# Third stage of a fused convolution block on one core: two tiling phases per chunk on TensorE, with six GELU buffers

## The chip, the cores and the metric

The kernel runs on one core of one Trainium2 chip. The metric is device time in microseconds. Before the change three runs took 3718.53, 3719.59 and 3721.88 us; the median is 3719.59 us. One further execution was recorded by the hardware profiler. All engines work in their own order of instructions: TensorE (PE, with its weight loads shown apart as PEld), VectorE (DVE), ScalarE (ACT), GpSimd (POOL) and SyncE (SP, which here only issues DMAs).

## The reference, cut to what matters

The input is 16 images of 192 channels and 64x64 pixels in float32. Layer 0 is a mixing block, layer 1 a convolution whose taps depend on the image:

```python
h = _ln2d(x, ln1_w, ln1_b)                      # layer norm over channels
projected, gate = split(conv1x1(h, in_proj_w))  # 192 -> 2 x 192
projected = dwconv3(projected, dw_k)
mixed = (directional_scan(projected) + dwconv3(projected, le_k)) * sigmoid(gate)
mixed = gelu(batch_norm(mixed))                 # statistics over all images
x = x + conv1x1(mixed, out_proj_w, out_proj_b)
h2 = _ln2d(x, ln2_w, ln2_b)
m = gelu(conv1x1(h2, fc1_w, fc1_b))             # 192 -> 768
x = x + conv1x1(m, fc2_w, fc2_b)                # 768 -> 192
# layer 1
pooled = x.mean(axis=(2, 3)); t = relu(norm(pooled @ w1.T)); wt = t @ w2.T + b2
out = depthwise_conv3(x, wt * MASK) + bias      # four taps are left by the mask
```

## The kernel before, in words

The kernel has three stages. The first projects x and writes the halves to DRAM, the second does the depthwise convolutions, the scans, the gate and the statistics of the batch norm. The third stage, which the change concerns, does the rest: the batch norm's GELU, the out projection with its residual, the second layer norm, the two products of the MLP, the pooling and layer 1.

The third stage works on pairs of images. Image 2p lies on partitions 0 to 63 and image 2p+1 on partitions 64 to 127; the 192 channels are three blocks t of 64. A chunk is 8 rows of 64 pixels, that is 512 pixels of each of the two images, so that a pair has 8 chunks (`NCH`) and all images together 64 (`n_ch`). Every engine's order is written out by hand (`tc.manual_schedule`); what stands in the loop is what each engine executes, in that order, and the framework only adds the semaphore waits that data and buffers require.

TensorE uses its array in two ways here. On quarters: weights of 64 rows and 64 columns, four products side by side, one for each combination of a 64-partition half of the input and a 64-partition half of the output. Over its full rows: weights of 128 rows and 64 columns, two products side by side. The products of one chunk n are these; a float32 matmul of the program is two MATMUL rows of the profile.

- `first` (line 980, quarters): fc1, 192 to 768 channels, six blocks m of 128 channels, 24 MATMUL rows each on 512 columns. A block goes to a PSUM tile of two banks with the tag `f1`, of which there are two; ScalarE applies the GELU to it (line 982) and writes a buffer `gl`, of which there are four.
- `second` (line 834, full rows): fc2, 768 to 192 channels, 36 pairs of MATMUL rows on 512 columns, accumulated over m into three PSUM banks with the tag `f2`.
- `out_quarters` (line 898, quarters) and `out_columns` (line 905, full rows): the out projection of channels 128 to 191 and 0 to 127 of chunk n+2, three blocks t of 8 MATMUL rows each on 256 columns. They go to half of an `f1` tile; `residual` (line 911, VectorE) adds x and the bias.
- `mean` (line 936, quarters): mean (`"sm"`) and mean square (`"sq"`) of chunk n+1 for the layer norm, 8 MATMUL rows each on 256 columns.

The loop runs over n. An iteration deals with chunk n in three rounds. Each round is `first(n, k)` on two blocks m, then `products(n, t)`, which takes one `f1` tile for one block t of the out projection of chunk n+2 and, for t 0 and 1, also for a mean of chunk n+1, and then one third of `second`. The third of `second` lags by one round, so that `second(n-1, 2)` stands in iteration n. Around these stand the other engines' steps: `center`, which subtracts the mean (VectorE, line 948); `squares`, one square on ScalarE (line 955) and five additions on VectorE (lines 956 and 928), into a buffer of its own; `normalize`, a square root on ScalarE with a table load before and after it (lines 964 and 966), a reciprocal (967) and a product (968) on VectorE; `final`, which adds fc2's result to the image (line 1000); `unmix`, three transposes on VectorE (line 239) of chunk n+3; `bn_gelu`, the batch norm's GELU on ScalarE (lines 861 and 862); `load` and `load_mixed`, DMAs that SP issues for chunks n+3 and n+4 (lines 204 and 227); and `piece`, called twice, which does one of the 12 output pieces of the pair that ended before (one activation on ScalarE, line 1039, three multiply-adds on VectorE, line 65, two DMAs on POOL, line 1043). After the last chunk of a pair, `pooled`, `squeeze` (line 1016) and `excite` (line 834, as `ps_k`) compute the taps of layer 1.

Of the kernel before, what the change touches and what calls it, by code (L numbers as in the profile page):

```python
# [21 lines left out]
F32 = mybir.dt.float32  # L22
# [33 lines left out]
def conv_block_kernel(ctx: ExitStack, tc: tile.TileContext, x, prm, w_in, w_out, w_fc1, b_fc1, w_fc2, w1, bn1, w2, out):  # L56
# [49 lines left out]
    pv = k2.tile([128, 2, NPRM], F32, tag="pv", name="pv")  # L106
# [58 lines left out]
    ones = ce.tile([128, 128], F32, tag="ones", name="ones")  # L165

# [697 lines left out]
    def products(n, t):  # L864


        if not -2 <= n < n_ch - 1:
            return
        ps = ps2.tile([128, 2, CH], F32, tag="f1", name="ps_o", bufs=2)
        pm, po = ps[:, :, HCH:CH], [ps[:, wh, 0:HCH] for wh in range(2)]  # L870
        if t < 2:
            at(mean, n + 1, pm, ("sm", "sq")[t])
        at(out_proj, n + 2, t, po)

        if t == 0:
            at(center, n + 1, pm)
        if t == 1 and 0 <= n + 1 < n_ch:
            st[n + 1]["pw"] = pm
        at(residual, n + 2, t, po)

# [12 lines left out]
    def out_quarters(n, t, ps, first_):  # L893
        s = st[n]

        for wh, qr in enumerate(HALF):
            for i, q in enumerate(HALF):
                nc.tensor.matmul(ps[wh][q], wo2[qr, 64 * t:64 * t + 64], s["mx"][qr, 2, 256 * i:256 * i + 256],  # L898
                                 start=first_, stop=not first_)

    def out_columns(n, t, ps, first_):
        s = st[n]
        for wh in range(2):
            for i, q in enumerate(HALF):
                nc.tensor.matmul(ps[wh][q].rearrange("p (r w) -> p r w", w=32), wo[:, 64 * t:64 * t + 64],  # L905
                                 cols(rows(s["mx"][:, i]))[:, :, wh], start=first_, stop=not first_)
# [23 lines left out]
    def mean(n, ps, what):  # L930


        s0, s1, sx = st[n][what]
        for k, kinds in enumerate(((s0, sx), (sx, s1))):
            for i, a in enumerate(kinds):
                nc.tensor.matmul(ps[HALF[i], k], mean64[HALF[k]], a[HALF[k]], start=True, stop=True)  # L936

    def mean_part(n, pm, t, k, src):

        for i, q in enumerate(HALF):  # L940
            nc.tensor.matmul(pm[q, k], mean64[q], src[q], start=(t == 0 and k == 0), stop=(t == 2 and k == 1))

    def center(n, pm):
        s, img = st[n], img_of(n)
        h = hp2.tile([128, 3, CH], F32, tag="h2", name="h2")
        hr = CR // 2
        for k in range(2):
            nc.vector.tensor_sub(h.rearrange("p t (h w) -> p t h w", w=HW)[:, :, k * hr:(k + 1) * hr], img[:, :, k * hr:(k + 1) * hr],  # L948
                                 rows(pm[:, k]).unsqueeze(1).broadcast_to([128, 3, hr, HW]))
        s.update(h=h)  # L950

    def squares(n):
        s = st[n]
        sq = wp.tile([128, 3, CH], F32, tag="sq2", name="sq2")
        nc.scalar.activation(sq, s["h"], AF.Square)
        nc.vector.tensor_add(sq[:, 0], sq[:, 0], sq[:, 1])
        v = sq.rearrange("p t (k n) -> p t k n", k=2)
        sums(v[:, 0, 0], v[:, 0, 1], v[:, 1, 0], v[:, 0, 0], v[:, 0, 1], v[:, 2, 0], v[:, 2, 1])
        s.update(sq=(v[:, 0, 0], v[:, 0, 1], v[:, 1, 0]))

    def normalize(n):
        s = st[n]
        rs = hp2.tile([128, CH], F32, tag="rs2", name="rs2", bufs=1)
        nc.scalar.activation(rs.rearrange("p (k n) -> p k n", k=2), s["pw"], AF.Sqrt, bias=eps6)  # L964

        nc.scalar.activation(warm, eps6, AF.Gelu)
        nc.vector.reciprocal(rs, rs)  # L967
        nc.vector.tensor_mul(s["h"], s["h"], rs.unsqueeze(1).broadcast_to([128, 3, CH]))  # L968

    def first(n, k):  # L970

        s = st[n]
        s["gl", k] = []
        for m in (2 * k, 2 * k + 1):
            pf = ps2.tile([128, 2, CH], F32, tag="f1", name="ps_f1", bufs=2)
            for t in range(3):
                for i, q in enumerate(HALF):
                    for j, o in enumerate(HALF):
                        m0 = 128 * m + 64 * j
                        nc.tensor.matmul(pf[o, i], wf1[q, t, m0:m0 + 64], s["h"][q, t], start=(t == 0), stop=(t == 2))  # L980
            gl = wp.tile([128, 2, CH], F32, tag="gl", name="gl", bufs=4)
            nc.scalar.activation(gl, pf, AF.Gelu, bias=bf1[:, m:m + 1])  # L982
            s["gl", k].append(gl)

    def second(n, k):
        s = st[n]
        if k == 0:
            s["po"] = [ps2.tile([128, CH], F32, tag="f2", name="ps_f2", bufs=3) for _ in range(3)]
        for j, gl in enumerate(s.pop(("gl", k))):
            m = 2 * k + j  # L990
            for t in range(3):
                both(s["po"][t], lambda i: wf2[:, m, 64 * t:64 * t + 64], lambda i: gl[:, i], m == 0, m == NFC - 1)
# [52 lines left out]
    def dynamic_last(p, g, t, dg, queues=(nc.gpsimd, nc.sync)):  # L1045
# [5 lines left out]
        else:  # L1051
            o = wp.tile([128, GR, HW], F32, tag="gl", name="ol", bufs=4)
# [36 lines left out]
    def out_alone(n, t, later=False):  # L1089

        if later:
            ps = [ps2.tile([128, CH], F32, tag="f2", name="ps_o2", bufs=3)[:, 0:HCH] for _ in range(2)]
# [8 lines left out]
    def one_bank():  # L1101
        return ps2.tile([128, 2, HCH], F32, tag="a", name="ps_m")
# [26 lines left out]
    load(2)  # L1129
    sq0 = wp.tile([128, 3, CH], F32, tag="sq2", name="sq2").rearrange("p t (k n) -> p k t n", k=2)  # L1130
# [8 lines left out]
    st[0]["pw"] = pw  # L1139
    normalize(0)  # L1140
# [4 lines left out]
    first(0, 0)  # L1145
    pm = ps2.tile([128, 2, CH], F32, tag="f1", name="ps_o", bufs=2)[:, :, 0:HCH]
    mean(1, pm, "sm")
    unmix(2)
    center(1, pm)
    bn_gelu(2)  # L1150
    squares(1)
    load(3)
    first(0, 1)
    unmix(3)
    out_alone(2, 0)
    second(0, 0)
    bn_gelu(3)
    products(0, 1)
    normalize(1)
    first(0, 2)  # L1160
    products(0, 2)
    second(0, 1)
    nc.vector.memset(pool2, 0.0)

    for n in range(1, n_ch + 1):
        ended = (n - 1) // NCH if n >= NCH and (n - 1) % NCH == NCH - 1 else None
        if n == 1:
            load_y(6, ys[3], (nc.gpsimd,))
        if n == NCH - 3:
            border(ximg[1])  # L1170
        at(load, n + 3)
        at(unmix, n + 3)
        at(load_mixed, n + 4)
        at(first, n, 0)
        at(bn_gelu, n + 3)
        products(n, 0)
        piece()
        at(squares, n + 1)
        at(second, n - 1, NPS - 1)
        at(final, n - 1)  # L1180
        if ended is not None:
            pooled(ended)
            if ended == n_pairs - 1:
                idle(2)
        at(first, n, 1)
        products(n, 1)
        if ended is not None:
            squeeze(ended)
        at(second, n, 0)
        piece()  # L1190
        at(normalize, n + 1)
        at(first, n, 2)
# [6 lines left out]
        products(n, 2)  # L1199
        at(second, n, 1)  # L1200

# [63 lines left out]
```

## Time and profile before

| | |
|---|---|
| runs | 3718.53, 3719.59, 3721.88 us (median 3719.59) |
| profiled execution, its own time | 3717.9 us |
| its span, first to last instruction | 3716.1 us |
| mean granted TensorE clock | 0.996 of full |
| busy: PE, DVE, ACT, POOL | 3693.1, 2700.6, 1784.8, 419.1 us |
| GELU on fc1's result (line 982) | 384 times, mean 1115 ns |
| first `first` of the third stage starts at | 1330.50 us |

How to read it: times are microseconds from the start of the span unless they are marked ns. A group of the page names line, engine, operation, the tile written, the tiles read, the shape and the count; then the busy time in total and the mean of one in ns, then the idle time of the engine just before these instructions and what ended most of it. "64\*64" in a MATMUL is the number of rows and columns of the array that it uses. A row of the timeline gives start, length, engine, line and operation of a run of equal instructions, and in brackets the idle time before it and what released it. Matmuls overlap: four quarter products that run side by side start some 7 ns apart, so starts, not lengths, tell what a group costs. What is true of a busy engine is not told by the share alone: a TensorE that is busy for 99% of the span can still lose time between two of its groups.

### The profile page before, as it was taken

How to read it: one execution, taken by the hardware profiler on the slowest of the kernel's cores; microseconds unless marked ns; L12 is line 12 of the kernel's file. 1: busy time of each engine (PE TensorE's matmuls, PEld its weight loads, DVE VectorE, ACT ScalarE, POOL GpSimd, SP SyncE). 2: the span in 40 equal slices, each digit the busy share in tenths (PEclk: the TensorE clock that was granted, in tenths of full speed). 3: DMA queues.
4: the chain of work that ended last, by engine and by line, in shares of the span. 5: the costliest groups of instructions: out<-in, count | busy, mean ns of one | idle time of the engine just before them, and what ended most of it. 6: DMA issues, size and time to landing. Idle time of an engine off the chain costs nothing.

```text
span 3716.1 us, 71125 instructions
## 1 busy us (share of the span) xinstructions
PE 3693.1 (99%) x30320; PEld 1649.0 (44%) x30320; DVE 2700.6 (73%) x4147; ACT 1784.8 (48%) x1940; POOL 419.1 (11%) x683
## 2 busy tenths in 40 slices
PE   9999999999999999999999999999999999999999
PEld 6666666555555533333333333333333333333333
DVE  7878776999999965557757756766675766675763
ACT  3334344888888843334434443434343443443433
POOL 3434342011011020000000000000000000000000
PEclk9999999999999999999999999999999999999999
DMA  7898997999999841112312222222222221221212
GB/s 170 253 253 247 262 282 259 284 297 283 283 281 271 225 101 39 40 44 69 84 48 68 72 62 67 63 65 64 72 57 62 77 68 46 78 74 43 69 38 74
DMA packets 289820, 491.80 MB, mean 132 GB/s; under 512 B 26456, under 2 KB 184144, under 8 KB 289504
## 3 DMA queue, kind: packets, MB, share of 16 engines
q1 hardware_dynamic: 232060, 296.09, 29.4%
q0 software_dynamic: 56512, 189.99, 18.5%
q8 instruction: 240, 3.93, 0.5%
q10 hardware_dynamic: 932, 1.16, 0.1%
q14 instruction: 76, 0.62, 0.1%
HBM read 284.95 MB, written 197.92 MB: 130 GB/s over the span
## 4 chain that ended last, share of the span: by engine, by line
PE 90%; DVE 1%; DMA 1%; ACT 0%; SPq 0%; issue 0%; POOL 0%; ACTq 0%; DVEq 0%
PE ps_f L980 27%; PE ps_f L834 27%; PE ps_l L668 11%; PE ps_pj L509 7%; PE ps_d L624 7%; PE ps_o L905 5%; PE ps_o L898 2%; PE ps_o L936 1%; PE ps_xt L480 1%; DMA xa<-in_x_dram 0%; PE ps_k L834 0%; PE ps_d L1067 0%; PE ps_i L1108 0%; DVE v L661 0%; PE pb_h L140 0%; DVE v L659 0%
## 5 line engine op out<-in xcount | busy, mean ns | idle before, releaser
L982 ACT ACTIVATE gl<-ps_f,bf 128x1024 f32<-128x1024 f32 x384 | 428.1, 1115 | 1318.1 <-PE ps_f L980 1318.1
L980 PE MATMUL ps_f<-h,wf 64*64 64x512 f32 x9216 | 1033.3, 593 | 3.0 <-DVE h L968 1.9
L834 PE MATMUL ps_f<-gl,place 128*64 128x512 f32 x4608 | 1022.2, 592 | 0.0
L980 PEld LDWEIGHTS ps_f<-h,wf 64*64 64x64 f32 x9216 | 333.6, 133 | 688.4 <-issue 633.7
L834 PEld LDWEIGHTS ps_f<-gl,place 128*64 128x64 f32 x4608 | 334.2, 137 | 574.5 <-issue 533.4
L509 PE MATMUL ps_pj<-wi,xa 64*128 64x384 f32 x3072 | 515.0, 487 | 1.1 <-DVE mid L514 0.9
L948 DVE TENSOR_TENSOR h<-ximg,ps_o 128x768 f32<-128x768 f32 x126 | 114.5, 950 | 420.7 <-PE ps_o L905 412.4
L509 PEld LDWEIGHTS ps_pj<-wi,xa 64*128 64x128 f32 x3072 | 292.1, 187 | 195.5 <-issue 10.6
L911 DVE SCALAR_TENSOR_TENSOR ximg<-ps_o,pt,low 128x256 f32<-128x256 f32 x384 | 167.8, 479 | 262.8 <-PE ps_o L905 259.1
L65 DVE SCALAR_TENSOR_TENSOR o<-ximg,taps,o 128x1024 f32<-128x1024 f32 x261 | 334.6, 1282 | 9.3 <-ACT o L1039 2.6
L1043 POOL DMA_DIRECT2D out_dram<-o x168 | 90.0, 541 | 2065.5 <-DVE o L65 2062.7
L967 DVE RECIPROCAL rs<-rs 128x512 f32<-128x512 f32 x64 | 214.3, 3349 | 28.6 <-ACT rs L964 28.6
L659 DVE TENSOR_TENSOR_SCAN v<-tab,q 128x1024 f32<-128x1024 f32 x96 | 218.3, 2274 | 7.8 <-DMA pg_d<-mid 7.8
L661 DVE TENSOR_TENSOR_SCAN v<-tab,q 128x1024 f32<-128x1024 f32 x96 | 217.5, 2265 | 0.0
L647 ACT ACTIVATE tab<-mask,dec_b 128x1024 f32<-128x1024 f32 x192 | 209.4, 1141 | 0.0
L905 PE MATMUL ps_o<-low,wo 128*64 128x256 f32 x1536 | 209.0, 393 | 0.0
L515 ACT ACTIVATE mid<-ps_pj,rsa 128x384 f32<-128x384 f32 x128 | 120.1, 939 | 185.0 <-PE ps_pj L509 176.6
L515 ACT ACTIVATE stg<-ps_pj,rsa 128x384 f32<-128x384 f32 x128 | 120.2, 941 | 179.0 <-PE ps_pj L509 172.5
L487 DVE BATCH_NORM_STATS2 st<-ps_xt 128x6 f32<-128x192 f32 x512 | 174.2, 340 | 11.8 <-PE ps_xt L480 10.9
L239 DVE STREAM_TRANSPOSE low<-low 128x512 f32<-128x512 f32 x174 | 167.8, 1016 | 2.1 <-issue 0.3
L1000 DVE SCALAR_TENSOR_TENSOR ximg<-ps_f,pt,ximg 128x512 f32<-128x512 f32 x192 | 134.4, 748 | 40.2 <-PE ps_f L834 37.8
L468 POOL DMA_DIRECT2D xa<-in_x_dram x192 | 119.8, 633 | 358.7 <-PE ps_pj L509 321.0
(210 smaller groups left out, 4050.4 us busy)
## 6 DMA issues: line engine op xcount, KB each, us to landing
low<-in_x_dram SPq DMA_DIRECT2D x128, 384.0 KB
out_dram<-o POOLq DMA_DIRECT2D x168, 256.0 KB, 3.7
mid<-pg_d SPq DMA_DIRECT2D x8, 4096.0 KB
low<-mixed_d SPq DMA_DIRECT2D x116, 256.0 KB
low<-pg_d SPq DMA_DIRECT2D x7, 4096.0 KB
pg_o<-pg_d SPq DMA_DIRECT2D x7, 4096.0 KB
xa<-in_x_dram POOLq DMA_DIRECT2D x192, 128.0 KB, 5.2
xa<-in_x_dram SPq DMA_DIRECT2D x192, 128.0 KB
```

Of the source, the lines that this page charges most:

```text
L65: nc.vector.scalar_tensor_tensor(o, in0, scalar, in1, ALU.mult, ALU.add, **kw)
L509: nc.tensor.matmul(ps[i], pixels(n, t, g)[q], wi[q, t].rearrange("p g k c -> p (g k c)"), start=(t == 0), stop=(t == 2))
L515: nc.scalar.activation(stag[blk][1][:, :, j], ps[1], AF.Copy, scale=rs[:, g, 1:2])
L624: nc.tensor.matmul(dst(ps[o, ih]), mats[g % 2]["dm"][q, di + 1, :, ch], src(s["pg"][q, :, 0, ch]), start=(di == 0), stop=stop)
L659: nc.vector.tensor_tensor_scan(vf, tab, q, 0.0, ALU.mult, ALU.add)
L661: nc.vector.tensor_tensor_scan(vf[:, ::-1], tab[:, ::-1], q[:, ::-1], 0.0, ALU.mult, ALU.add)
L668: nc.tensor.matmul(dst(bst[k]["ps"][o, i]), lm_of(g)[q, m, :, c], src(q, ih), start=start, stop=stop)
L834: nc.tensor.matmul(ps[q], w(i), rhs(i), start=start, stop=stop)
L905: nc.tensor.matmul(ps[wh][q].rearrange("p (r w) -> p r w", w=32), wo[:, 64 * t:64 * t + 64], cols(rows(s["mx"][:, i]))[:, :, wh], start=fi ...
L967: nc.vector.reciprocal(rs, rs)
L980: nc.tensor.matmul(pf[o, i], wf1[q, t, m0:m0 + 64], s["h"][q, t], start=(t == 0), stop=(t == 2))
L982: nc.scalar.activation(gl, pf, AF.Gelu, bias=bf1[:, m:m + 1])
```

## The change

An iteration of the loop becomes two phases. First all products on quarters: `first` for m 0 and 1, `mean` "sm" of chunk n+1, `first` for m 2 to 5, `mean` "sq", and `out_quarters` of chunk n+2 for all three t. Then all products over the full rows: `out_columns` for all three t, and the whole `second` of the same chunk n. `final(n-1)` stands at the head of the iteration, `normalize`, `residual` and `bn_gelu` stand between the phases, and `load`, `load_mixed` and `unmix` move behind the blocks of `first`.

Buffers go with it. `gl` has six buffers instead of four. The means no longer share an `f1` tile with the out projection; each takes two of the three `f2` banks (`two_banks`), and the square root is done in two halves. The out projection takes two `f1` tiles at once: t 0 and t 1 in the first halves of two tiles, t 2 in the second half of the first. The squares go to the x2 buffer of their chunk (`x2s[n % 2]`) instead of a buffer of their own, so that `load(n+3)` comes after the mean of the squares; `pv` moves to a pool that is closed before the third stage.

```diff
-    def products(n, t):
...
-        ps = ps2.tile([128, 2, CH], F32, tag="f1", name="ps_o", bufs=2)
-        pm, po = ps[:, :, HCH:CH], [ps[:, wh, 0:HCH] for wh in range(2)]
-        if t < 2:
-            at(mean, n + 1, pm, ("sm", "sq")[t])
-        at(out_proj, n + 2, t, po)
-
-        if t == 0:
-            at(center, n + 1, pm)
-        if t == 1 and 0 <= n + 1 < n_ch:
-            st[n + 1]["pw"] = pm
-        at(residual, n + 2, t, po)
...
     def squares(n):
         s = st[n]
-        sq = wp.tile([128, 3, CH], F32, tag="sq2", name="sq2")
+
+        sq = x2s[n % 2]
         nc.scalar.activation(sq, s["h"], AF.Square)
...
-        nc.scalar.activation(rs.rearrange("p (k n) -> p k n", k=2), s["pw"], AF.Sqrt, bias=eps6)
+        for k in range(2):
+            nc.scalar.activation(rs[:, k * HCH:(k + 1) * HCH], s["pw"][k], AF.Sqrt, bias=eps6)
...
-    def first(n, k):
+    def first(n, m):
...
+        pf = ps2.tile([128, 2, CH], F32, tag="f1", name="ps_f1", bufs=2)
+        for t in range(3):
+            for i, q in enumerate(HALF):
+                for j, o in enumerate(HALF):
+                    m0 = 128 * m + 64 * j
+                    nc.tensor.matmul(pf[o, i], wf1[q, t, m0:m0 + 64], s["h"][q, t], start=(t == 0), stop=(t == 2))
+        gl = wp.tile([128, 2, CH], F32, tag="gl", name="gl", bufs=6)
+        nc.scalar.activation(gl, pf, AF.Gelu, bias=bf1[:, m:m + 1])
+        s["gl", m] = gl
...
+    def two_banks(name):
+        return [ps2.tile([128, CH], F32, tag="f2", name=name, bufs=3)[:, 0:HCH] for _ in range(2)]
...
-    for n in range(1, n_ch + 1):
+    for n in range(n_ch + 1):
         ended = (n - 1) // NCH if n >= NCH and (n - 1) % NCH == NCH - 1 else None
-        at(load, n + 3)
-        at(unmix, n + 3)
-        at(load_mixed, n + 4)
-        at(first, n, 0)
-        at(bn_gelu, n + 3)
-        products(n, 0)
-        piece()
-        at(squares, n + 1)
-        at(second, n - 1, NPS - 1)
         at(final, n - 1)
...
+        at(first, n, 0)
         at(first, n, 1)
-        products(n, 1)
+        if n + 1 < n_ch:
+            pm = two_banks("ps_m")
+            mean(n + 1, pm, "sm")
+            center(n + 1, pm)
+        at(first, n, 2)
+        at(squares, n + 1)
+        for m in range(3, NFC):
+            at(first, n, m)
+        if n == 0:
+            unmix(2)
+            bn_gelu(2)
+        at(unmix, n + 3)
+        at(load_mixed, n + 4)
+        piece()
+        if n + 1 < n_ch:
+            st[n + 1]["pw"] = two_banks("ps_v")
+            mean(n + 1, st[n + 1]["pw"], "sq")
+        at(load, n + 3)
+        po = []
+        if n + 2 < n_ch:
+
+            pair = [ps2.tile([128, 2, CH], F32, tag="f1", name="ps_o", bufs=2) for _ in range(2)]
+            po = [[pair[j][:, wh, c0:c0 + HCH] for wh in range(2)] for j, c0 in ((0, 0), (1, 0), (0, HCH))]
+            for t in range(3):
+                out_quarters(n + 2, t, po[t], True, t < 2)
         if ended is not None:
             squeeze(ended)
+        for t in range(len(po)):
+            out_columns(n + 2, t, po[t], False, t > 0)
+        at(normalize, n + 1)
+        for t in range(len(po)):
+            residual(n + 2, t, po[t])
+        at(bn_gelu, n + 3)
         at(second, n, 0)
-        piece()
-        at(normalize, n + 1)
-        at(first, n, 2)
         if ended is not None:
             excite(ended)
...
-        products(n, 2)
         at(second, n, 1)
+        piece()
+        at(second, n, 2)
```

The lines ahead of the loop that did the first chunk apart are gone; the loop now begins at n = 0.

## The prediction

> **What bounds the kernel now.** I read the page first: shares, chain and groups.
>
> ```profile
> PE 3693.1 (99%) x30320; PEld 1649.0 (44%) x30320; DVE 2700.6 (73%) x4147; ACT 1784.8 (48%) x1940; POOL 419.1 (11%) x683
> ...
> PE 90%; DVE 1%; DMA 1%; ACT 0%; SPq 0%; issue 0%; POOL 0%; ACTq 0%; DVEq 0%
> ...
> L982 ACT ACTIVATE gl<-ps_f,bf 128x1024 f32<-128x1024 f32 x384 | 428.1, 1115 | 1318.1 <-PE ps_f L980 1318.1
> L980 PE MATMUL ps_f<-h,wf 64*64 64x512 f32 x9216 | 1033.3, 593 | 3.0 <-DVE h L968 1.9
> L834 PE MATMUL ps_f<-gl,place 128*64 128x512 f32 x4608 | 1022.2, 592 | 0.0
> ```
>
> TensorE is the chain, and in the third stage it waits for nobody: 3.0 us before all of `first`, nothing before `second`. So whatever an edit moves on VectorE, ScalarE or the queues counts only where it makes TensorE wait; and what can be saved must lie between TensorE's own groups. The timeline of TensorE in a chunk of the steady part shows what lies there.
>
> ```profile
> 2399.94 5.32 PE L834 MATMUL ps_f<-gl,place 128*64 128x512 f32 x24
> 2405.19 5.38 PE L980 MATMUL ps_f<-h,wf 64*64 64x512 f32 x48
> 2410.39 0.61 PE L936 MATMUL ps_o<-sq,mean 64*64 64x256 f32 x8
> 2410.82 0.61 PE L898 MATMUL ps_o<-low,wo 64*64 64x256 f32 x8
> 2411.36 1.08 PE L905 MATMUL ps_o<-low,wo 128*64 128x256 f32 x8
> 2412.28 5.32 PE L834 MATMUL ps_f<-gl,place 128*64 128x512 f32 x24
> ...
> 2436.52 4.03 PE L834 MATMUL ps_f<-gl,place 128*64 128x512 f32 x18
> ```
>
> Read start to start. A chunk takes 2436.52 - 2399.94 = 36.58 us. What do the groups cost without a change of tiling? The end of the stage, where two thirds of `second` follow each other, tells it:
>
> ```profile
> 3655.38 5.37 PE L834 MATMUL ps_f<-gl,place 128*64 128x512 f32 x24
> ...
> 3665.99 10.52 PE L834 MATMUL ps_f<-gl,place 128*64 128x512 f32 x48
> ```
>
> The second 24 rows add 5.15 us (0.429 a pair). In the steady part `second` takes 5.25 to the start of `first`: 0.10 more, at the change from full rows to quarters. `first`, whose 12 fours have the same pace, takes 5.20 to the mean that follows on quarters: 0.05 more, and the trace's starts put it between its first and second four (460 ns instead of 409). The mean takes 0.43, but `out_quarters`, equally large, 0.54: 0.11 at the change to full rows; `out_columns` then has 0.91 for four pairs of 0.215, another 0.05. A round trip between the two tilings therefore costs 0.10 + 0.05 + 0.11 + 0.05 = 0.31 us (0.312 with the trace's nanoseconds), three times a chunk. Check: 36.58 - 3 x 0.312 = 35.65, and 6 x 5.15 + 5 x 0.43 + 3 x 0.86 = 35.63.
>
> [...] after each change the first load starts together with its matmul and the next four is 0.05 late. The same would hold after any stop, and the one below shows it. [...] a block of `first` takes 2.57 us, its GELU 1.115. [...]
>
> **The change, part by part.** *Fewer changes of tiling.* In the order of TensorE's instructions I count the round trips in the third stage: 197 before (3 x 64, and 5 ahead of the loop), 76 after (64, the same 5, and 7 because `excite`, on quarters, now stands inside `second`). 121 x 0.312 = 37.8 us less. No matmul is added or left out.
>
> *A new wait in every chunk.* `f1` has two tiles. Blocks m 4 and m 5 of `first` fill the first and the second; then `out_quarters` wants the first for t 0 and the second for t 1. Between the last block and t 1 TensorE has only the mean (0.43) and t 0 (0.43). Call E the start of that mean. t 1 could start at E + 0.86, but the GELU of m 5 must have read the tile. The kernel before has this situation once, in its first chunk, where a block of `first` follows a single mean; the timeline of all engines there:
>
> ```profile
> 1335.70 0.61 PE L936 MATMUL ps_o<-sm,mean 64*64 64x256 f32 x8
> 1335.95 1.11 ACT L982 ACTIVATE gl<-ps_f,bf 128x1024 f32<-128x1024 f32 x1 [1.46 <-PE ps_f L980]
> ...
> 1337.11 5.38 PE L980 MATMUL ps_f<-h,wf 64*64 64x512 f32 x48 [0.80 <-ACT gl L982]
> ```
>
> TensorE resumes 1.41 us after the mean's start, 0.05 after the GELU's end. In the steady chunks the GELU starts a little later, since it waits for two semaphores:
>
> ```profile
> 2410.70 1.12 ACT L982 ACTIVATE gl<-ps_f,bf 128x1024 f32<-128x1024 f32 x1 [1.46 <-PE ps_f L980]
> ```
>
> That is E + 0.31 with E = 2410.39, so t 1 starts at E + 0.31 + 1.115 + 0.05 = E + 1.475. TensorE stands for 1.475 - 0.86 = 0.61 us, plus the 0.05 of a late second weight load: 0.66 a chunk. Nothing is done meanwhile: t 2, whose tile is free, and `out_columns` are queued behind t 1. Chunks 1 to 61 have it: 61 x 0.663 = 40.4 us. Bounds: with the faster start of the first chunk (0.25 instead of 0.31) and no late load it is 0.55, 33.6 us; with 0.1 us more it is 46.5. I take 40.4.
>
> *First chunk.* Its `bn_gelu(2)` stands behind the last GELU on ScalarE, and `out_quarters` needs it. In the trace the two activations end 1.83 us after the GELU before them, so the quarters start at E + 1.42 + 1.83 + 0.05 = E + 3.31 instead of E + 0.43: 2.9 us. The chunk before had stops of 1.03 (above) and 0.56 (TensorE resumes at 1356.82 instead of 1356.26, behind another GELU) which go. Net +1.3.
>
> *Chunk 62* has no out projection between the mean of the squares and `second`, and `second`'s second bank is the one that the square root reads. ScalarE has the GELU (to E + 1.42), the activation of the last piece (1.23, starting 0.1 early), the table load (1.28) and the root's first half: E + 4.33, of which I put 0.47 for half of a root that takes 0.69 whole. `second` wants the bank at E + 0.97: +3.4.
>
> *Where the same bank costs nothing:* in chunks 0 to 61 t 1 and t 2 of the quarters, 2.6 us of `out_columns` and the first pair of `second` lie between; the bank is wanted at E + 5.57 and the root's halves end at E + 4.3 and E + 4.8. With 1.2 us less of that cover each chunk would pay for what is missing.
>
> *VectorE*, chunk with pieces, from the chunk's start: the second piece of the chunk before ends 0.4 late, three `final` (0.83 each) end at 3, the mean asks for their banks at 5.25. `center` 6.1 to 7.9, square on ScalarE behind the third GELU to 11.1, five additions (0.69 + 1.77) to 13.6; the mean of the squares comes at E = 15.96: 2.3 spare. Transposes (2.9) to E + 0.6, piece (3.9) from E + 2.6 to E + 6.5, reciprocal 3.35 and product 1.76 to E + 11.7, residuals with their sums 5.3 to E + 17. The next chunk starts at E + 20.7, so that 3.7 are spare for its `f1` tiles and 9 for `h`; one more piece there would use up the 3.7. The square doesn't hold up the GELU of m 3, which can start only at 11.13.
>
> *Queues.* On SP `load(n+3)` goes behind `load_mixed`, eight DMAs whose issue takes 12.7 us, and behind the mean of the squares; it is used at E + 48. POOL's two DMAs a piece are the same. Splitting the root costs two fixed parts, 0.2 once ahead of the loop where nothing covers it (0 to 0.7). `pv` and the squares' buffer cost nothing: no instruction changes.
>
> Sum: -37.8 + 40.4 + 1.3 + 3.4 + 0.2 = +7.6 us. The profiled execution took 3717.9 us, 1.7 less than the median of the runs, so it is 3725.5 for that execution and 3719.6 + 7.6 = 3727.2 for the median.
>
> **The rivals.** *The wait is not there, or is hidden* (ends faster). If the GELU of m 5 were through by E + 0.86, only the other terms would count: 3719.6 - 37.8 + 4.9 = 3686.7. It decides in the time from the last block to t 1's tile: each 0.1 us less is 6.1 us, and below 0.42 of stop the kernel is faster by more than 0.2%. For it: the GELU's length and TensorE's resuming come from few places. Against: in 378 of the 384 cases ScalarE starts 0.72 after the block's last four starts, which is E + 0.31, and 0.61 of what follows would have to vanish. 8 in 100.
>
> *Another engine becomes late* (clearly slower). ScalarE or VectorE is behind in the chunks with pieces, 6 of 8, so that `second` waits for the root as well: past the 1.2 us of cover above, each 0.5 us more makes 46 x 0.5 = 23 us, 3750. For it: VectorE has 27 us of work in these chunks and a piece now stands ahead of the reciprocal. Against: the schedule above, where every meeting point has 1.2 us or more. 12 in 100.
>
> *The change doesn't do what it says*: the order of the changed program shows the two phases, so I give it nothing.
>
> **How the numbers follow.** The forecast has 80 in 100 and by itself lies between 3720 (the short wait, 0.55) and 3733 (the long one). 0.2% is 7.4 us, about what a measurement of this kernel can tell from no change, and the forecast's centre lies on it: of its 80, 38 fall within 0.2% and 42 slower. With the rivals: faster 8, within 38, slower 54. The range 3715 to 3741 holds the forecast's own and the beginning of the late-engine case.
>
> **What would show it.** Right: chunks of about 36.6 us as before; in each one 5 us long run of `out_columns` and `second` without a break; a new entry in the list of waits, TensorE at `ps_o` (`out_quarters`) for the GELU, 61 times some 0.6 us, 37 us in all; one wait of 3 us at chunk 0 and one at chunk 62 for the root. Wrong: no such entry and chunks of 35.96 us (first rival); TensorE waiting in `second` for the root, or for VectorE at a mean or `h`, in more than a chunk or two (second); or a round trip that costs something else where it is left, at `second` to `first` and at `out_quarters` to `out_columns`.

## The result, and the profile after

The changed kernel takes 3727.65 us (median of 13 runs, 3723.15 to 3731.02) where the kernel before takes 3718.56 us (median of 13, 3714.61 to 3721.88). The ratio of the times is 1.0023, with a 95% interval of 1.0016 to 1.0031: slower by a quarter of a per cent. The forecast was 3727.2, with 3715 to 3741 as its range. The medians differ by 9.1 us, where the prediction's sum gives 7.6; the interval, 5.9 to 11.5 us, holds both.

The page of the changed kernel, shares, chain and three of its groups (lines 963, 965 and 834 are `first`, its GELU and `second`):

```profile
PE 3666.2 (99%) x30320; PEld 1677.6 (45%) x30320; DVE 2703.6 (73%) x4147; ACT 1792.3 (48%) x2004; POOL 418.2 (11%) x683
...
PE 88%; ACT 2%; DVE 1%; issue 1%; DMA 0%; SPq 0%; ACTq 0%; POOL 0%; DVEq 0%
...
L965 ACT ACTIVATE gl<-ps_f,bf 128x1024 f32<-128x1024 f32 x384 | 427.4, 1113 | 1340.6 <-PE ps_f L963 1334.6
L963 PE MATMUL ps_f<-h,wf 64*64 64x512 f32 x9216 | 1014.9, 590 | 2.0 <-DVE h L953 2.0
L834 PE MATMUL ps_f<-gl,place 128*64 128x512 f32 x4608 | 1001.9, 592 | 2.8 <-ACT rs L949 2.8
```

TensorE's busy time fell by 26.9 us, from 3693.1 to 3666.2, and yet the execution is longer. ScalarE, at 0% of the chain before, now holds 2% of it. `second`, which waited for nobody, has one wait of 2.8 us. Which instruction waits for ScalarE the rest of the time is told by the list of TensorE's waits (tile, line, releaser: total us, times, longest):

```profile
PE ps_o L881 <- ACT gl L965: 26.3, 61, 0.4
...
PE ps_f L834 <- ACT rs L949: 2.8, 1, 2.8
PE ps_o L881 <- ACT low L862: 2.6, 1, 2.6
```

The out projection on quarters (line 881) waits for the GELU in 61 chunks; that is the entry that the prediction named, with its count. The other two are chunk 62 and chunk 0. The list has 0.4 us a time where the stop is 0.6, because it measures from the end of the matmul before, and that end is modelled some 0.2 us late. The starts tell it. TensorE's timeline in the chunk that corresponds to the one shown of before:

```profile
2400.11 5.38 PE L963 MATMUL ps_f<-h,wf 64*64 64x512 f32 x48
2405.31 0.61 PE L919 MATMUL ps_m<-sm,mean 64*64 64x256 f32 x8
2405.74 10.48 PE L963 MATMUL ps_f<-h,wf 64*64 64x512 f32 x96
2416.04 0.61 PE L919 MATMUL ps_v<-low,mean 64*64 64x256 f32 x8
2416.47 0.61 PE L881 MATMUL ps_o<-low,wo 64*64 64x256 f32 x8
2417.52 1.09 PE L881 MATMUL ps_o<-low,wo 64*64 64x256 f32 x16 [0.43 <-ACT gl L965]
2418.54 2.81 PE L888 MATMUL ps_o<-low,wo 128*64 128x256 f32 x24
2421.18 15.62 PE L834 MATMUL ps_f<-gl,place 128*64 128x512 f32 x72
2436.73 3.66 PE L963 MATMUL ps_f<-h,wf 64*64 64x512 f32 x32
```

A chunk takes 2436.73 - 2400.11 = 36.62 us; before it took 36.58. There is one change to full rows (2418.54) and one back (2436.73) where there were three of each. Between t 0 of the quarters (2416.47) and t 1 (2417.52) lie 1.05 us for work of 0.43, so TensorE stands for 0.62. ScalarE in the same place:

```profile
2416.35 1.11 ACT L965 ACTIVATE gl<-ps_f,bf 128x1024 f32<-128x1024 f32 x1 [1.46 <-PE ps_f L963]
2417.36 1.23 ACT L1022 ACTIVATE o<-ximg,pt,taps 128x1024 f32<-128x1024 f32 x1
...
2419.91 0.84 ACT L949 ACTIVATE rs<-ps_v,eps 128x256 f32<-128x256 f32 x2
```

The GELU of m 5 starts 0.31 us after the mean, ends at 2417.46, and t 1 starts 0.06 later. So in 61 chunks two round trips between the tilings were exchanged for one stop of nearly the same price: 36.583 - 2 x 0.312 + 0.663 = 36.622, which is what the chunk takes in the trace's nanoseconds.

Two executions are best compared from the first `first` of the third stage on, since what lies ahead of it ended between 1328.7 and 1336.2 us in the executions of this study, while its work differs by the split root alone. From there to the end the kernel before takes 2385.6 us and the changed one 2392.7: 7.1 more. By the prediction it is 7.4, its 7.6 less the 0.2 of the split root, which lies ahead of the loop.

### The profile page after: what moved, and what is told of

It reads as the page before. It is cut to its first block, busy times and chain, and to the rows that moved or that the text cites. A ratio compares the mean times of both kernels' runs of the same rounds, so it can differ in the third digit from the quotient of the medians.

```text
span 3721.4 us, 71304 instructions
## 1 busy us (share of the span) xinstructions
PE 3666.2 (99%) x30320; PEld 1677.6 (45%) x30320; DVE 2703.6 (73%) x4147; ACT 1792.3 (48%) x2004; POOL 418.2 (11%) x683
## 4 chain that ended last, share of the span: by engine, by line
PE 88%; ACT 2%; DVE 1%; issue 1%; DMA 0%; SPq 0%; ACTq 0%; POOL 0%; DVEq 0%
PE ps_f L963 27%; PE ps_f L834 27%; PE ps_l L668 11%; PE ps_pj L509 7%; PE ps_d L624 7%; PE ps_o L888 5%; PE ps_o L881 2%; ACT gl L965 2%; PE ps_xt L480 1%; PE ps_m L919 1%; PE ps_k L834 0%; PE ps_d L1050 0%; DMA out_dram<-ol 0%; PE ps_i L1095 0%; DVE v L661 0%
## 5 line engine op out<-in xcount | busy, mean ns | idle before, releaser
L963 PE MATMUL ps_f<-h,wf 64*64 64x512 f32 x9216 | 1014.9, 590 | 2.0 <-DVE h L953 2.0
L834 PE MATMUL ps_f<-gl,place 128*64 128x512 f32 x4608 | 1001.9, 592 | 2.8 <-ACT rs L949 2.8
L963 PEld LDWEIGHTS ps_f<-h,wf 64*64 64x64 f32 x9216 | 346.3, 133 | 627.9 <-issue 566.0
L931 DVE TENSOR_TENSOR h<-ximg,ps_m 128x768 f32<-128x768 f32 x128 | 116.4, 951 | 278.5 <-PE ps_m L919 277.3
L940 DVE TENSOR_TENSOR low<-low 128x512 f32<-128x512 f32 x63 | 43.6, 692 | 212.0 <-ACT low L939 212.0
L888 PE MATMUL ps_o<-low,wo 128*64 128x256 f32 x1536 | 181.6, 384 | 0.0
```

The lines of the kernel that those rows point to most:

```text
L834: nc.tensor.matmul(ps[q], w(i), rhs(i), start=start, stop=stop)
```

## The experiments

All kernels of this section are the changed kernel with the edit shown (of "no wait" and "all waits" a part, with the rest in words), and compute the whole reference. "Chunk" is the time from one `first` of m 0 to the next in the middle of the stage; "stage" is from the first `first` to the end of the profiled execution, of which there is one for each kernel. "E" is, as in the prediction, the start of the mean of the squares. The intervals are against runs of the kernel before on the same chip.

| kernel | us, median (lowest to highest, runs) | against before, 95% | chunk | stage |
|---|---|---|---|---|
| before | 3718.56 (3714.61 to 3721.88, 13) | | 36.583 | 2385.6 |
| changed | 3727.65 (3723.15 to 3731.02, 13) | 1.0023 (1.0016 to 1.0031) | 36.622 | 2392.7 |
| t 1 last | 3703.68 (3700.76 to 3709.73, 4) | 0.9962 (0.9947 to 0.9977) | 36.190 | 2368.3 |
| t 1 first | 3727.82 (3723.92 to 3731.61, 10) | 1.0025 (1.0015 to 1.0034) | 36.62 | 2392.8 |
| mean last | 3754.71 (3751.59 to 3756.89, 4) | 1.0096 (1.0079 to 1.0112) | 37.053 | 2421.2 |
| no wait | 3684.62 (3681.43 to 3685.01, 4) | 0.9907 (0.9892 to 0.9922) | 35.960 | 2351.9 |
| three trips | 3727.76 (3723.13 to 3731.73, 12) | 1.0023 (1.0015 to 1.0032) | 36.583 | 2392.4 |
| batch norm ahead | 3742.13 (3738.65 to 3743.83, 4) | 1.0062 (1.0047 to 1.0077) | 36.90 or 36.62 | 2407.0 |
| chunk 0 alone | 3725.76 (one run) | | 36.62 | 2390.9 |
| all waits | 3677.43 (3671.34 to 3681.70, 4) | 0.9888 (0.9873 to 0.9902) | 35.960 | 2345.1 |

The theory: TensorE takes its matmuls in the order written, and one stop before t 1 gives back what fewer changes of tiling save. The first question is whether the stop sets the time, which a stop of another length answers, and whether a round trip costs 0.31 us, which a kernel with a different number of trips answers. The rival: something else in the two phases (the order of VectorE, a late buffer) keeps the chunk at 36.6 us, and the wait is only where TensorE is seen to idle; then the time moves on to the next wait when this one is shortened.

### t 1 last

```diff
-            for t in range(3):
+            for t in (0, 2, 1):
                 out_quarters(n + 2, t, po[t], True, t < 2)
```

t 2 uses the second half of t 0's tile, so it can go ahead of t 1 and covers 0.43 us of the GELU.

> The order of the out projection's quarters is t 0, t 2, t 1 instead of t 0, t 1, t 2. Theory (a fixed wait for the GELU of block m 5): t 1 is reached 0.43 us later, at E + 1.29 instead of E + 0.86, and still released at E + 1.475, so the stop shrinks from 0.61 to 0.18 us a chunk: 61 x 0.43 = 26 us less than the changed kernel's 3727.7, that is 3701, ratio to the kernel before 0.9955. Rival (the tilings' round trips never cost what the trace suggests and the wait only takes place of another loss): no change beyond noise, 3727.

The chunk takes 36.190 us, 0.432 less. The list of waits has no entry for line 881 and the GELU any more; the timeline of TensorE shows what is left of the stop:

```profile
2405.97 0.61 PE L919 MATMUL ps_v<-low,mean 64*64 64x256 f32 x8
2406.40 1.71 PE L881 MATMUL ps_o<-low,wo 64*64 64x256 f32 x24
2408.03 2.81 PE L888 MATMUL ps_o<-low,wo 128*64 128x256 f32 x24
```

The 24 rows take 1.63 us to the next group, where three times 0.43 and the 0.11 of the change to full rows are 1.40. A stop of 0.18 and 0.05 of a late weight load are still in it, too short for the list because of the modelled ends. One line's order is worth 61 x 0.432 = 26.4 us, of which 1.7 were lost again at chunk 62 in the profiled execution (last section; 24.4 in the stage); the kernel is now faster than before. The rival falls for this step: nothing else caught the time.

### t 1 first

```diff
-            for t in range(3):
+            for t in (1, 0, 2):
                 out_quarters(n + 2, t, po[t], True, t < 2)
```

> The order of the quarters is t 1, t 0, t 2. Theory: t 1 is reached at E + 0.43 and released at E + 1.475, a stop of 1.04 us a chunk, 61 x 0.43 = 26 us more than the changed kernel: 3754, ratio to before 1.0095. Rival: 3727.

This expectation was missed, and the trace says why: the edit did nothing. TensorE's timeline:

```profile
2424.17 0.61 PE L881 MATMUL ps_o<-low,wo 64*64 64x256 f32 x8
2425.22 1.09 PE L881 MATMUL ps_o<-low,wo 64*64 64x256 f32 x16 [0.43 <-ACT gl L965]
```

There are eight rows without a wait, then the same wait, and 16 rows. So the tile that is written first had the buffer that came free first, that of m 4, whatever its name is. This fits a pool that gives out a buffer when a tile is first used and not when it is asked for; the profile shows no addresses, so it is read from the waits. The two tiles were renamed, not exchanged. What it gives is a repeat of the changed kernel, 1.0025. To lengthen the stop, something else had to be taken from its cover.

### Mean last

```diff
             st[n + 1]["pw"] = two_banks("ps_v")
-            mean(n + 1, st[n + 1]["pw"], "sq")
-        at(load, n + 3)
...
             for t in range(3):
                 out_quarters(n + 2, t, po[t], True, t < 2)
+        if n + 1 < n_ch:
+            mean(n + 1, st[n + 1]["pw"], "sq")
+        at(load, n + 3)
```

The mean of the squares, 0.43 us, stands behind the quarters, so that only t 0 lies between m 5 and t 1.

> In the run with t 1 first the tile of block m 5 was still the one used second, since a buffer is given out at its first use; so that run was the changed kernel under other names. Here the mean of the squares, 0.43 us, moves behind the quarters of the out projection, and the second tile is reached 0.43 us earlier. Theory: the stop grows from 0.61 to 1.04 us a chunk, 61 x 0.43 = 26 us more than the changed kernel: 3754, chunks of 37.05 us, ratio to before 1.0095. The rival, that the position in the queue doesn't matter: 3727.

The list of waits and the timeline of TensorE:

```profile
PE ps_o L881 <- ACT gl L965: 52.6, 61, 0.9
```

```profile
2432.12 0.61 PE L881 MATMUL ps_o<-low,wo 64*64 64x256 f32 x8
2433.59 1.09 PE L881 MATMUL ps_o<-low,wo 64*64 64x256 f32 x16 [0.86 <-ACT gl L965]
```

Between the first two starts lie 1.47 us, again 0.43 of work, so the stop is 1.04. The chunk takes 37.053 us, 0.431 more than in the changed kernel. Together with "t 1 last" and the changed kernel this is a dose: stops of 0.18, 0.61 and 1.04 us give chunks of 36.190, 36.622 and 37.053.

### No wait

```diff
-            pair = [ps2.tile([128, 2, CH], F32, tag="f1", name="ps_o", bufs=2) for _ in range(2)]
-            po = [[pair[j][:, wh, c0:c0 + HCH] for wh in range(2)] for j, c0 in ((0, 0), (1, 0), (0, HCH))]
-            for t in range(3):
+            pair = ps2.tile([128, 2, CH], F32, tag="f1", name="ps_o", bufs=2)
+            po = [[pair[:, wh, c0:c0 + HCH] for wh in range(2)] for c0 in (0, HCH)]
+            po.insert(1, two_banks("ps_o1"))
+            for t in (1, 0, 2):
                 out_quarters(n + 2, t, po[t], True, t < 2)
```

t 1 goes to two `f2` banks instead of m 5's tile, t 0 and t 2 to m 4's tile. For this the mean of the squares takes one `f2` bank and one bank that was idle; and since `second` needs the `f2` banks soon, `out_columns` and `residual` begin with t 1, and the first `piece` goes behind that residual. No matmul, activation or transfer is added.

> t 1 of the out projection goes to two f2 banks instead of the second f1 tile, comes first, and its residual is done first; the mean of the squares takes one f2 bank and the bank with the tag a. Theory: no wait for the GELU in any chunk, chunks of 35.96 us, 61 x 0.663 = 40.4 us less than the changed kernel: 3687, ratio to before 0.9915. The first bank of the second product is now the root's; it is wanted at E + 4.47 and free at E + 4.38, so at most a few tenths of a us in the 42 chunks with a piece may come back. Rival (the saved round trips were worth less than 0.312 us each): the kernel lands at the time before, 3719.

```profile
2400.83 1.48 PE L881 MATMUL ps_o<-low,wo 64*64 64x256 f32 x24
2402.23 2.81 PE L888 MATMUL ps_o<-low,wo 128*64 128x256 f32 x24
2404.87 15.62 PE L834 MATMUL ps_f<-gl,place 128*64 128x512 f32 x72
```

The timeline has the 24 rows at 1.40 us, nothing between them, and `second` follows at once; the list of waits has no entry for the GELU. The chunk takes 35.960 us, 0.662 less than in the changed kernel: 0.61 of stop and 0.05 of late weight load, the two parts that the prediction gave it. 61 x 0.662 is 40.4, and the wait for the root at chunk 62 became 0.9 shorter as well; the stage is 40.8 us shorter, and the medians differ by 43.0, which is the same within the intervals. The saving of the two round trips is there in full when the stop is gone, 1.0% in all.

### Three trips

```diff
             for t in range(3):
                 out_quarters(n + 2, t, po[t], True, t < 2)
+                out_columns(n + 2, t, po[t], False, t > 0)
         if ended is not None:
             squeeze(ended)
-        for t in range(len(po)):
-            out_columns(n + 2, t, po[t], False, t > 0)
```

Each t goes through both of its tilings before the next, so that the chunk has three round trips again. t 1 is then wanted 1.56 us after t 0's first row, which hides the GELU. Quarters and columns of a t follow each other as in the kernel before; all else is as in the changed kernel.

> The changed kernel with out_columns of each t right behind its out_quarters: three round trips a chunk again instead of one, and t 1 is reached only after the first out_columns, at E + 1.9, after its tile is free. Theory: + 2 x 0.312 us for the trips, - 0.663 us for the wait, so -0.04 us x 61 = 2 us less than the changed kernel: 3725, ratio to before 1.0017. If the trips cost nothing: 3687. If the wait were not what the GELU makes it: 3766.

```profile
2418.25 0.61 PE L881 MATMUL ps_o<-low,wo 64*64 64x256 f32 x8
2418.79 1.08 PE L888 MATMUL ps_o<-low,wo 128*64 128x256 f32 x8
2419.81 0.66 PE L881 MATMUL ps_o<-low,wo 64*64 64x256 f32 x8
```

The changes cost what they did in the kernel before: 0.54 for the eight quarter rows with the change to full rows, 1.02 for four pairs with the way back. The chunk takes 36.583 us, 0.623 more than without a wait and with one trip. Both of these kernels wait for nobody in a steady chunk, and two trips are the difference: 0.312 each. So the price of a trip, read from the gaps of the kernel before, holds here too.

The two prices now stand measured apart. Two trips cost 0.623 us, the stop 0.662. The change gains the first and pays the second.

### Batch norm ahead of the root

```diff
+        at(bn_gelu, n + 3)
         at(normalize, n + 1)
         for t in range(len(po)):
             residual(n + 2, t, po[t])
-        at(bn_gelu, n + 3)
```

This tests the second rival of the prediction, a late root. The cover is the time between the end of the root's first half and the moment at which `second` wants that bank. The two activations of `bn_gelu` here stand ahead of the root and take from it. The expectation already counts with a cover of 6.0 - 4.33 = 1.67 us instead of the prediction's 1.2, for a reason told below.

> The changed kernel with the batch norm's GELU of chunk n+3 (1.93 us on ScalarE) ahead of the square root instead of behind it. Theory, from the changed kernel's own trace: the root's first half ends at E + 4.33 with a piece ahead of it; now at E + 6.26, and the second product wants the bank at E + 6.0, so it stops for 0.26 us and 0.05 of wake-up and 0.05 of a late load in the 41 chunks with a piece there, none in the others: 15 us more than the changed kernel, 3742, ratio to before 1.0065. Rival (ScalarE already is at the edge, so that all 1.93 us come through in these chunks): 3807. Rival (ScalarE has ample room): 3727.

ScalarE's timeline, and TensorE's in the same chunk:

```profile
1686.88 1.23 ACT L861 ACTIVATE low<-low,bn_bi,bn_sc 128x1024 f32<-128x1024 f32 x1
...
1688.83 1.28 ACT L949 ACT_TABLE_LOAD   x1
1690.12 0.84 ACT L949 ACTIVATE rs<-ps_v,eps 128x256 f32<-128x256 f32 x2
```

```profile
1689.57 15.90 PE L834 MATMUL ps_f<-gl,place 128*64 128x512 f32 x72
```

`second` takes 15.90 us instead of 15.62: a stop of 0.23 and 0.05 of a late load are inside it. The first half of the root ends at E + 6.18 instead of E + 4.34, 1.84 later, and TensorE goes on at E + 6.23 where the changed kernel wants the bank at E + 6.00. So the cover in the changed kernel is 6.00 - 4.34 = 1.66 us, and it doesn't wait there. The expected 0.36 was too large by 0.08, because it moved the root by 1.93. The chunks with both a piece and a batch norm ahead of the root take 36.90 us, the others 36.62, since without the piece's 1.23 us there is room. There are 40 of them, not the 41 expected: chunk 61 has a piece, but no batch norm. Of the 14.3 us by which the stage is longer, 40 x 0.28 = 11.2 are this; 1.7 lie in chunk 62 and 1.3 at the end, both from TensorE's clock (last section).

### Chunk 0 alone

```diff
             mean(n + 1, pm, "sm")
+            if n == 0:
+                unmix(2)
             center(n + 1, pm)
...
             at(first, n, m)
-        if n == 0:
-            unmix(2)
-            bn_gelu(2)
+            if n == 0 and m == 3:
+                bn_gelu(2)
```

In the changed kernel chunk 0 cost more than the prediction gave it. This edit lets chunk 2's transposes and batch-norm GELU run earlier, so that chunk 0 has no stop for them and its products are the same.

> The changed kernel with the batch norm's GELU of chunk 2 between the blocks of first of chunk 0, nothing else. Chunk 0 of the changed kernel takes 40.33 us: 2.8 of stop and some 1.4 more, in which the products after the stop run at half their pace. Theory (a stop of 2.6 us lowered the clock for 3.4 us): without the stop both go and chunk 0 takes 36.62 us like the others. Rival (the slow products have another cause, such as the DMAs at that time): it takes 38.0.

Chunk 0 takes 36.564 us instead of 40.33. The quarters follow the mean without the wait for line 862:

```profile
1349.06 0.61 PE L919 MATMUL ps_v<-low,mean 64*64 64x256 f32 x8
1349.49 0.61 PE L881 MATMUL ps_o<-low,wo 64*64 64x256 f32 x8
1350.48 1.09 PE L881 MATMUL ps_o<-low,wo 64*64 64x256 f32 x16 [0.37 <-ACT gl L965]
```

The quarters start 2.82 us earlier after the mean (0.43 instead of 3.25). From their start to `second` it is 4.65 us instead of 5.60, although 0.61 for the stop behind the GELU, late load included, is now in it: 1.56 us were lost by the clock in the changed kernel, which is 0.50 there for 3.41 us (the section on the prediction shows it); here the same rows take 4.65 - 0.61 = 4.04 us, as in "all waits". The expected rival, another cause of the slow products, would have left chunk 0 at 38.0. The one execution took 3725.76 us, within the spread of the changed kernel: 1.9 us of the gain are lost again at its end, where the clock fell in this execution and not in the changed kernel's.

### All waits

The edits of "no wait" and "chunk 0 alone", and for chunk 62:

```diff
+            if n + 2 < n_ch:
...
+            else:
+                last_pw = ps2.tile([128, 2, CH], F32, tag="f1", name="ps_v", bufs=2)
+                st[n + 1]["pw"] = [last_pw[:, k, 0:HCH] for k in range(2)]
...
+        piece()
         at(bn_gelu, n + 3)
```

The last mean of the squares goes to an `f1` tile, which no out projection needs then, and the first `piece` goes behind the residuals in all chunks.

> The kernel without the wait (3684.6 us) with three more moves: the batch norm's GELU of chunk 2 between the blocks of first of chunk 0, the mean of the squares of the last chunk in an f1 tile, and the piece behind the residuals instead of ahead of the root. Theory: chunk 0 falls from 40.5 to about 36.0 us, chunk 62 from 34.2 to 32.1, the others stay at 35.96: 6.6 us less, 3678, ratio to before 0.989. If the stop of chunk 0 was not the whole of its 4.5 us: 3680.

Chunk 62 takes 32.07 us instead of 35.06, and chunk 0 takes 35.96. TensorE's timeline at the end:

```profile
3593.71 0.61 PE L919 MATMUL ps_v<-low,mean 64*64 64x256 f32 x8
3594.25 15.67 PE L834 MATMUL ps_f<-gl,place 128*64 128x512 f32 x72
```

`second` follows the mean at once. The stage is 47.6 us shorter than in the changed kernel; 61 x 0.662 + 4.37 + 2.99 = 47.7. This is the best version of the study: 1.1% faster than the kernel before, with the same matmuls, activations and transfers.

## Why the prediction was right, and where not

**The price of a round trip, 0.31 us: right.** Three trips against one, without any wait in either kernel, differ by 2 x 0.312. That is the price for float32 between these two tilings.

**The new wait, 0.66 us in 61 chunks: right.** t 1 starts at E + 1.48 (1.475 by the prediction); the list of waits has the 61 entries; taking the stop away gives back 0.662. Only one of its signs is off: the unbroken run of `out_columns` and `second` is 18.2 us long (2418.54 to 2436.73), not 5. The value came from the only place of the kernel before where a block of `first` met a single mean, moved by the 0.06 us by which a steady GELU starts later (E + 0.31 for E + 0.25; the trace of before has a semaphore instruction of ScalarE's queue at 380 of the 384 GELUs, at none of the four that start before 1343 us). The forecast had taken the later start and the late load, not the 0.55 of its lower bound, which would have given 3720. The late load is in the changed kernel's trace too: behind the stop at 2417.52 the second four weight loads start 0.05 us after the first four matmuls, and the second four matmuls 0.27 us after the first, where the next follow at 0.22. One PSUM tile a chunk is emptied too late for TensorE: t 1's, by 0.62 us.

**The excite's trip: half a microsecond too dear.** A chunk in which `excite` stands takes 38.53 us, 1.906 more than the others; before it was 1.665 more. The extra trip costs 0.24, not 0.31, seven times.

**The first chunk: net +1.3 by the prediction, 2.8 measured.** The wrong term is the one it didn't have. The start of the quarters was right: E + 3.25, with E + 3.31 predicted. But what came then ran at another speed. TensorE's timeline in chunk 0 of the changed kernel, and then three stretches of 3.41 us there (stretch: length, busy time of PE, PEld, DVE, ACT and POOL with counts, granted clock, DMA share, GB/s):

```profile
1344.59 0.61 PE L919 MATMUL ps_v<-low,mean 64*64 64x256 f32 x8
1347.84 2.84 PE L881 MATMUL ps_o<-low,wo 64*64 64x256 f32 x24 [2.63 <-ACT low L862]
1350.61 3.00 PE L888 MATMUL ps_o<-low,wo 128*64 128x256 f32 x24
```

```profile
1344.20:1347.61 3.41, 1.01 (x16) 0.27 (x8) 3.41 (x4) 2.77 (x3) 0.00 (x0) 1.00 0.52 158
1347.62:1351.03 3.41, 3.19 (x26) 1.59 (x28) 1.30 (x2) 3.36 (x5) 0.00 (x0) 0.50 0.79 163
1351.03:1354.44 3.41, 3.41 (x30) 1.96 (x28) 3.38 (x2) 2.25 (x4) 0.00 (x0) 1.00 0.00 0
```

The granted clock is 1.00 up to the end of the stop, 0.50 for the next 3.41 us and 1.00 after them. The 24 rows of the quarters take 2.77 us to the next group, 1.40 in the kernel without a wait. The prediction priced a stop by its length alone; here it had also to pay for the work behind it.

**Chunk 62: +3.4 by the prediction, 3.0 measured.** All engines' timeline there:

```profile
3632.18 0.61 PE L919 MATMUL ps_v<-low,mean 64*64 64x256 f32 x8
...
3632.72 1.08 PE L834 MATMUL ps_f<-gl,place 128*64 128x512 f32 x4
...
3636.04 0.84 ACT L949 ACTIVATE rs<-ps_v,eps 128x256 f32<-128x256 f32 x2
3636.57 14.81 PE L834 MATMUL ps_f<-gl,place 128*64 128x512 f32 x68 [2.77 <-ACT rs L949]
```

TensorE resumes at E + 4.39; the prediction's 4.33 and 0.05 give 4.38. But it had stopped later: `second` does four MATMUL rows, two pairs, on its first bank before it wants the second one, since a float32 product is two rows. The bank is wanted at E + 1.45 (0.54 for the mean with the change to full rows, and 0.86 + 0.05 for two pairs and a late load), not at E + 0.97, which counted one pair.

**The cover of the root, 1.2 us: too small by the same slip.** With two pairs on the first bank the cover is 0.43 us more than the prediction's 5.57 - 4.33 = 1.24, and "batch norm ahead" measured 1.66. The second rival, for which the prediction had 12 in 100 and a limit of 1.2, was therefore further off than it said; and a piece stands ahead of the root in 42 chunks, from the second pair on, not in the 46 of its price. Neither count had a part in the forecast's sum.

**The split root ahead of the loop: right.** It takes 0.84 us there, in two activations of 0.47 that overlap by 0.1, instead of 0.69 in one: 0.15 of the 0.2 predicted.

**VectorE's schedule: right where it matters.** No mean and no `h` waits for VectorE in a steady chunk, in the changed kernel and in those without a stop, which leave VectorE 0.66 us less a chunk.

The sum of the stage: chunks 1 to 61 gave +4.0 (by the prediction 61 x 0.039 and 7 x 0.312, 4.6), chunk 0 +2.8 (1.3) and chunk 62 +3.0 (3.4). Trips saved in chunks 0 and 62 and in the last one gave -1.9, as counted. The end of the kernel behind the last `second` is 0.8 shorter, where the clock fell in the kernel before and not in the changed one's profile (last section). That is 7.1, against 7.4. The two large terms, -37.8 and +40.4, were right to within half a microsecond each. The small ones were off by up to 1.5 us, and that they nearly cancel is luck: the clock at chunk 0 cost 1.5 that the prediction had at nothing, and the shorter stop at chunk 62, the cheaper trips of `excite` and the end of the kernel gave back about 1.7.

Whether the result falls within 0.2% or is slower, the prediction left nearly open, since its centre lay on that limit. It lies just past it, 1.0023, and the interval of 1.0016 to 1.0031 holds both sides.

## What to carry to other kernels

When a reorder gathers work of one kind, ask which buffer the first instruction behind the gathered block wants, and who empties it: here the last block of `first` is emptied with only 0.86 us of work left to cover it. Look then for independent work or another buffer to stand there (here t 2 before t 1 gave 24 us, and two other banks for t 1 gave 41 to 43), and check by the order of first use which instruction really gets the early buffer. Look at the granted clock of what follows a stop before pricing the stop by its length (here the one of 2.6 us at chunk 0 cost 1.56 us more in the matmuls behind it, at a clock of 0.50), and count how many MATMUL rows stand on the first bank before the second one is wanted.

## What the runs showed of the hardware that was not expected

Behind a stop of TensorE of 2.6 us the granted clock was 0.50, and of stops of 2.77 us some were followed by it and some were not. At chunk 0, the stop of 2.6 us in the list of waits (3.1 in "mean last") was followed by slow matmuls in the profiles of all seven kernels that have it, at a cost of 1.5 to 1.7 us; in the changed kernel the clock was 0.50 for 3.41 us. In the five of them in which 24 rows of quarters and then 24 of columns follow the stop, these take 5.54 to 5.74 us up to `second`; in "all waits", which doesn't have the stop, they take 4.04. "Chunk 0 alone" doesn't have it either, and has no slow matmuls there.

At chunk 62, a stop of 2.77 us was followed by a slow stretch in three profiles (t 1 last, three trips, batch norm ahead) and by none in four (the changed kernel, t 1 first, mean last, chunk 0 alone). The same 68 rows of `second` with the same wait, in the timeline of "t 1 last":

```profile
3612.25 16.51 PE L834 MATMUL ps_f<-gl,place 128*64 128x512 f32 x68 [2.77 <-ACT rs L949]
```

They took 14.81 in the changed kernel: 1.70 us for the clock alone. From their start to the next group it is 14.74 us in each of the four and 16.25 to 16.44 in the three. A stretch of 3.4 us of these rows, with the columns shown for chunk 0, first in "t 1 last" and then in the changed kernel:

```profile
3612.60:3616.00 3.40, 3.40 (x10) 0.98 (x8) 3.36 (x3) 1.47 (x2) 1.07 (x2) 0.50 0.08 19
```

```profile
3637.97:3641.38 3.41, 3.41 (x20) 1.12 (x18) 3.41 (x2) 0.41 (x2) 1.07 (x2) 1.00 0.36 79
```

The clock is 0.50 in the one and 1.00 in the other, behind stops of 2.77 us in both. What decides between them is left open here. The shorter stop of 1.9 us at chunk 62 of "no wait" was not followed by slow matmuls (13.89 us from there to the next group), and neither were the 61 stops of 0.6 us (and of 1.04 in "mean last"): those chunks are alike to 0.02 us, and in the changed kernel the clock is 1.00 in the one shown (2416.47 to 2418.54).

At the very end, behind the excite's products of one column and waits of 0.62 and 0.27 us, the clock was 0.50 in four profiles (the kernel before, mean last, batch norm ahead, chunk 0 alone); in the kernel before this is the stretch from 3682.90 to 3685.00. It stayed at 1.00 in the other six, in the changed kernel from 3688.50 to 3692.00. This is 0.8 to 1.9 us of the stage that no edit made.
